# A graph kernel's last layer: source rows of three in seven cell groups fetched by indirect DMA in place of one-hot matmuls

## The chip, the cores and the metric

The kernel runs on one core of a Trainium2 chip. The metric is the device time of one execution in microseconds (us). The core has a matrix engine (TensorE, PE), a vector engine (VectorE, DVE), an activation engine (ScalarE, ACT), a general engine (GpSimd, POOL) and a queue engine (SyncE, SP). PE reads its operands from the on-chip memory SBUF and writes PSUM. DMA queues move data between DRAM and SBUF; SP, ACT and POOL issue them, and only POOL issues the indirect ones that fetch rows by index.

## What is computed

Four graph layers run one after the other on 3125 nodes of 128 features and 103125 edges (50000 random pairs in both directions, and a loop on each node). Each adds its result to x. The change is in the last:

```
h = relu(layernorm(x))
comp  = h[src] + rel_emb[rel_id]                 # one row of 128 per edge
score = sum(comp * h[dst], axis=-1)
smax  = segment_max(score, dst);  ex = exp(score - smax[dst])
norm  = ex / segment_sum(ex, dst)[dst]
neigh = segment_sum(comp * norm[:, None], dst)
x = x + tanh(neigh @ neigh_w)
```

All values are float32.

## The kernel before

**Cells.** The nodes are cut into T = 28 tiles of Q = 112. An edge belongs to the cell (tile of its source, tile of its target). Each cell has 128 slots, one per SBUF partition; edges beyond 128 go to OV = 3 overflow slots per partition of the target tile. `lay_out` sorts the edges into cells at the program's start. There `own` holds, for each slot, the source node's number in its tile, or -1 for an empty slot. `kind` and `rel` are further columns of the same layout, sent to DRAM or kept.

**Columns and groups.** The last layer works through 28 columns, one per target tile. A column has NG = 8 groups: seven groups of K = 4 cells (4 x 128 edges), and a last one that holds the overflow's 3 x 128 edges. `attend` does this, for the first layer (three hops) and for the last (one hop). Every group passes through the same steps:

- `s_load` (L800): the load of half a column's slot numbers, copied to 112 partitions (L774). `s_hot` (L826): DVE turns them into a one-hot matrix.
- `s_rel` (L834): SP loads the group's 4 x 128 relation rows (256 KB).
- `s_rows` (L836): PE makes the source rows. The features are kept as three bfloat16 parts whose sum is the float32 value, so each cell takes three matmuls, and a group 12 (L845). The rows land in a PSUM tile `pg`, of which there are two. For the overflow group the rows come from `over_rows` instead.
- `s_comb` (L853): DVE adds the relation rows, giving `v`.
- `s_turn` (L861, copied by ACT in L863): PE transposes v. `s_score` (L877): PE multiplies by the targets' features; DVE masks the product in L879, with `other` made by ACT (L1626) from `eq`, loaded by SP (L1621).
- `s_most` (L891): DVE keeps the running maximum of the column. After the last group PE turns it (L899), DVE reduces it and puts it on a diagonal (L905 to L908), PE spreads it over the partitions (L917) and ACT copies it (L919).
- `s_less` (L923, DVE), `s_exp` (L927, ACT) and `s_sum` (L935, PE): subtract the maximum, exponential, weighted sum of v per target.
- After a column: division (L1630 to L1634); after four columns a product with `neigh_w` (L1642), tanh, addition to x and the store of the output.

**Order.** The order of the work is written out by hand. The list `order` at the end of `attend` gives each step a delay in groups: at iteration i the step with delay d works on group i - d, and the steps of one iteration stand in the order of the list. `in_order` ties each engine's instructions to this order. So within an iteration PE does L935 (delay 21), L917 (11), L899 (10), L877 (8), L861 (6) and L845 (4). DVE does L923 (19), L891 (9), L853 (5), L879 (8), L905 to L908 (10) and L826 (2). `s_load` has delay 0.

**Gathers.** Where a row is fetched by index, `gather` (L708) has POOL issue an indirect DMA: 128 rows of 512 bytes, one for each partition. Before the change the last layer has three of them per column, for the overflow's rows (`s_over`, L814), 84 in all, into two buffers `orow`. They come from the table `rows_d` in DRAM, which SP writes from the normalised features at the layer's start (L1615). In the first layer's second and third hop POOL also fetches the relation rows for the last layer (`rel_ahead`, the tile `ahead`) and writes them to DRAM (L1012).

Of the kernel before, what the change touches and what calls it, by code (L numbers as in the profile page):

```python
# [7 lines left out]
F32 = mybir.dt.float32  # L8
BF16 = mybir.dt.bfloat16
FP16 = mybir.dt.float16  # L10
I32 = mybir.dt.int32
AF = mybir.ActivationFunctionType
OP = mybir.AluOpType
# [3 lines left out]
P = 128  # L17
D = 128
H, C = 4, 32
K = 4  # L20
# [3 lines left out]
Q = 112  # L24
# [418 lines left out]
def by_cells(ctx: ExitStack, tc: tile.TileContext, edges, x, E, edge_emb, q_w, k_w, Ws, Wd, att_s, att_d,  # L443
# [9 lines left out]
    nc = tc.nc  # L453
    N = x.shape[0]
    T = -(-N // Q)
# [5 lines left out]
    NG = T // K + 1  # L461
# [78 lines left out]
    overO = node.tile([P, 2, T, OV], F32, name="overO")  # L540
    n_src = node.tile([Q, T], F32, name="n_src")
    inO = node.tile([P, T, OV], I32, name="inO")
    slots_o = tc.dram_tile([2 * T * NO, 4], F32, name="slots_o")

    def rows_out(rb, to, width, by_dst):
# [11 lines left out]
    def lay_out(rows, tab, pp, pname):  # L557
# [11 lines left out]
        with tc.tile_pool(name="lay", bufs=1) as lp:  # L569
# [11 lines left out]
            for i in range(4):  # L581
                c = slice(i * W // 4, (i + 1) * W // 4)
# [3 lines left out]
            def flat(name, dtype=F32, n=W):  # L586
                return lp.tile([P, n], dtype, name=name)

            def split(f, bits):

                v = flat(f"v{f}")
                for j in range(2):
                    c = slice(j * WH, (j + 1) * WH)
                    nc.vector.tensor_add(v[:, c], layC[:, c, f], tab[2 * f + j][:, :WH])
                i = flat(f"i{f}", I32)
                nc.vector.tensor_scalar(i, v, 2.0 ** bits, None, op0=OP.mult)
                lo, hi = flat("lo", I32), flat("hi", I32)
                nc.vector.tensor_single_scalar(hi, i, bits + 7, op=OP.arith_shift_right)
                nc.vector.tensor_single_scalar(lo, i, bits, op=OP.arith_shift_right)
                hf, lf, at = flat(f"hf{f}"), flat(f"lf{f}"), flat(f"at{f}")  # L600
                nc.scalar.copy(hf, hi)
                nc.vector.tensor_scalar_add(lf, lo, -1.0)
                nc.vector.scalar_tensor_tensor(at, hf, -128.0, lf, op0=OP.mult, op1=OP.add)
                return v, i, hf, lf, at

            def row_tiles(f):

                n = f.shape[-1]
                w = min(n, Q)
                rb = lp.tile([w, n // w, P], BF16, name=f"rb{n}", bufs=2)  # L610
                for i0 in range(0, n // w, K):
                    m = min(K, n // w - i0)
                    pt = pp.tile([P, K, P], F32, name=pname)
                    for i in range(m):
                        nc.tensor.transpose(pt[:w, i, :], f[:, (i0 + i) * w:(i0 + i + 1) * w], ident)
                    nc.scalar.copy(rb[:, i0:i0 + m, :], pt[:w, :m, :])
                return rb

            def over_out(rb, to):
                o = bass.AP(tensor=to.tensor, offset=to.offset + T * P, ap=[[COL * P, T], [P, OV], [1, P]])  # L620
                nc.sync.dma_start(o, rb[:, 0, :])
# [8 lines left out]
            v0, _, k0, l0, own = split(0, 11)  # L630
# [8 lines left out]
            rows_out(row_tiles(kind[:, :NC]), src_kind, COL, False)  # L639
            over_out(row_tiles(kind[:, NC:]), src_kind)  # L640


            rel = flat("rel")
            nc.vector.tensor_sub(rel, v0, l0)
# [62 lines left out]
    def gather(to, table, index):  # L707
        return nc.gpsimd.indirect_dma_start(out=to, out_offset=None, in_=table,  # L708
                                            in_offset=bass.IndirectOffsetOnAxis(ap=index, axis=0))
# [4 lines left out]
    def norm_relu_steps(h):  # L714

        st = work.tile([Q, T, 6], F32, name="bn", bufs=1)
        mv = work.tile([Q, T, 2], F32, name="mv", bufs=1)
        for n0, n1 in quads():
            for n in range(n0, n1):
                nc.vector.bn_stats(st[:, n, :], xs[:, n, :])  # L720
                nc.vector.bn_aggr(mv[:, n, :], st[:, n, :])
            yield
        rs = work.tile([Q, T], F32, name="rs", bufs=1)
        nc.scalar.activation(rs, mv[:, :, 1], AF.Sqrt, bias=eps[:Q])
        nc.vector.reciprocal(rs, rs)
        for n0, n1 in quads():
            for n in range(n0, n1):
                nc.vector.tensor_scalar(h[:, n, :], xs[:, n, :], mv[:, n, 0:1], rs[:, n:n + 1],
                                        op0=OP.subtract, op1=OP.mult)
            nc.scalar.activation(h[:, n0:n1, :], h[:, n0:n1, :], AF.Relu)  # L730
            yield

    def norm_relu(h):
        for _ in norm_relu_steps(h):
            pass
# [41 lines left out]
    def width(g):  # L777
        return OV if g == NG - 1 else K


    def attend(oh_d, tables, idx, side, combine, rel_d, masks, finish, rel_rows=None, right=None, aside=None,
               column_end=None, extra=None):

# [7 lines left out]
        hop = 0  # L793
# [6 lines left out]
        def s_load(c, g):  # L800
            s = st[c, g] = {}
            m = width(g)
            if g % H1 == 0:
                h = cols[c, g // H1] = {}
                h["n"] = min(HALF if g == 0 else COL - HALF, T - g * K)
                h["oh"] = row_tile(oh_d, c, g * K, h["n"], name="oh")
            if g == 0:
                over_rows[c] = work.tile([P, OV, D], F32, name="orow", bufs=2)
            if rel_rows and not hop:
                rel_rows[0](s, c, g)  # L810
            if aside:
                aside(c * NG + g)

        def s_over(early, late):  # L814

# [20 lines left out]
        def s_rows(c, g):  # L836
            s, h = st[c, g], cols[c, g // H1]
            e0 = g % H1 * K
            if g == NG - 1:
                s["rows"] = over_rows.pop(c)  # L840
            else:
                pg = s["rows"] = pg_.tile([P, K, D], F32, name="pg")
                for k in range(K):
                    for i in range(3):
                        nc.tensor.matmul(pg[:, k, :], h["oh"][:, (e0 + k) * P:(e0 + k + 1) * P],  # L845
                                         parts[:, g * K + k, i, :D], start=(i == 0), stop=(i == 2))
            if rel_rows and not hop:
                rel_rows[2](s, c, g)
# [104 lines left out]
        with in_order(tc):  # L953
            for i in range(len(tables) * A - AFTER + 1 + order[0][1]):
                for f, d in order:
                    hop, u = divmod(i - d, A)
                    if 0 <= hop < len(tables) and u < T * NG:
                        f(*divmod(u, NG))
                hop, u = divmod(i, A)
# [12 lines left out]
    hop = 0  # L972
# [25 lines left out]
    with tc.tile_pool(name="work0", bufs=3) as work:  # L998
# [96 lines left out]
        tables = rows_d, rows_e, rows_d  # L1095
# [513 lines left out]

    with tc.tile_pool(name="work3", bufs=3) as work:  # L1610
        h = big.tile([Q, T, D], F32, name="agg")
        norm_relu(h)
        for n0, n1 in quads():
            in_parts(h, n0, n1)
        nc.sync.dma_start(node_rows(rows_d), h)  # L1615
        side = work.tile([P, T, Q], F32, name="side", bufs=1)
        sides(h, side)
        def other_load(s, c, g):
            m = width(g)
            s["eq"] = work.tile([P, K, Q], F32, name="eq", bufs=4)  # L1620
            nc.sync.dma_start(s["eq"][:, :m, :].rearrange("p k q -> p (k q)"), eq_d[c * NG + g, :, :m * Q])  # L1621

        def other_make(s, c, g):
            m = width(g)
            s["other"] = work.tile([P, K, Q], BF16, name="other", bufs=4)
            nc.scalar.activation(s["other"][:, :m, :], s["eq"][:, :m, :], AF.Copy, bias=1.0, scale=-1.0)  # L1626

        def weight(c, acc):
            r = over_one[c] = work.tile([Q, 1], F32, name="r", bufs=2)
            nc.vector.tensor_scalar_max(r, acc[:, D:D + 1], 1e-30)  # L1630
            nc.vector.reciprocal(r, r)

        def mean(c, acc):
            nc.scalar.activation(h[:, c, :], acc[:, :D], AF.Copy, scale=over_one.pop(c))  # L1634

        def turned(n0, n1):
            nexts[n0] = transposed(h, n0, n1)

        def by_w(n0, n1):
            pw = pm.tile([P, K, P], F32, name="pm")  # L1640
            for n in range(K):
                nc.tensor.matmul(pw[:Q, n, :], nexts[n0][:, n, :], nw, start=True, stop=True)  # L1642
            nexts[n0] = work.tile([Q, K, D], F32, name="th", bufs=2)
            nc.scalar.activation(nexts[n0], pw[:Q], AF.Tanh)

        def result(n0, n1):
            nc.vector.tensor_add(xs[:, n0:n1, :], xs[:, n0:n1, :], nexts.pop(n0))
            n = n1 - (n1 == T)
            nc.sync.dma_start(out[n0 * Q:n * Q, :].rearrange("(n p) d -> p n d", p=Q), xs[:, n0:n, :])
            if n1 == T:  # L1650
                nc.sync.dma_start(out[n * Q:, :], xs[:TAIL, n, :])

        attend(dst_oh, (rows_d,), inO, side, OP.add, dst_rel, (other_load, other_make, lambda *a: None),
               (weight, mean, *map(by_quads, (turned, by_w, result))))


@with_exitstack
# [701 lines left out]
```

## Time and profile before

| | |
|---|---|
| median of 3 runs | 7348.25 us (7346.42 to 7352.07) |
| profiled execution | 7342.68 us |
| its span, first to last instruction | 7340.9 us |
| mean granted TensorE clock | 0.913 |
| PE, DVE, ACT, POOL busy over the span | 85%, 75%, 52%, 50% |
| last layer | from about 6652 us to the end |
| gathers of the last layer (L708, orow) | 84, first 6678.9, 0.938 / 0.944 / 1.187 us (least, median, most) |

The page's shares are means over the whole program, of which the last layer is a tenth. So what follows is read in windows of that layer. In a table by windows each engine has its busy time and, in brackets, its number of instructions; then come the granted clock, the share of time in which the core's DMA engines were busy, and GB/s. In a timeline each row has the start, the duration, the engine, the line, the operation with output and inputs, and in brackets how long the engine sat idle before it and what ended this. A float32 matmul is recorded as two, so "x8" stands for four. DVE's and PE's operations overlap at their ends, so the time from one start to the next is what one costs in a train of them. In the list of waits each row has the total in us, the number of waits and the longest.

### The profile page before, as it was taken

How to read it: one execution, taken by the hardware profiler on the slowest of the kernel's cores; microseconds unless marked ns; L12 is line 12 of the kernel's file. 1: busy time of each engine (PE TensorE's matmuls, PEld its weight loads, DVE VectorE, ACT ScalarE, POOL GpSimd, SP SyncE). 2: the span in 40 equal slices, each digit the busy share in tenths (PEclk: the TensorE clock that was granted, in tenths of full speed). 3: DMA queues.
4: the chain of work that ended last, by engine and by line, in shares of the span. 5: the costliest groups of instructions: out<-in, count | busy, mean ns of one | idle time of the engine just before them, and what ended most of it. 6: DMA issues, size and time to landing. Idle time of an engine off the chain costs nothing.

```text
span 7340.9 us, 161470 instructions
## 1 busy us (share of the span) xinstructions
PE 6244.2 (85%) x59495; PEld 5200.1 (71%) x59495; DVE 5521.5 (75%) x12113; ACT 3838.1 (52%) x12186; POOL 3688.5 (50%) x3346
## 2 busy tenths in 40 slices
PE   5887739999999999999967777777877777988999
PEld 3443328888888888888856666666776776767999
DVE  8887638888866667777767878879997997237887
ACT  3666514444544445444556676655665666114555
POOL 2677767776568876888823333323342232341110
PEclk9787769999999999999978888888897898999999
DMA  2100025555467776766756766677777786556665
GB/s 65 26 19 17 12 62 150 149 149 150 146 193 207 204 207 185 206 204 200 205 168 204 213 209 212 210 203 204 209 209 195 209 210 179 146 150 185 211 210 170
DMA packets 695243, 1222.75 MB, mean 167 GB/s; under 512 B 129530, under 2 KB 459680, under 8 KB 694444
## 3 DMA queue, kind: packets, MB, share of 16 engines
q1 hardware_dynamic: 575340, 996.40, 46.1%
q0 software_dynamic: 109120, 208.86, 11.8%
q8 instruction: 473, 7.75, 0.5%
q10 hardware_dynamic: 9984, 7.07, 0.3%
q14 instruction: 326, 2.67, 0.1%
HBM read 915.61 MB, written 296.27 MB: 165 GB/s over the span
## 4 chain that ended last, share of the span: by engine, by line
PE 59%; DVE 10%; ACT 8%; DMA 4%; issue 3%; POOL 1%; ACTq 0%; SPq 0%; DVEq 0%; POOLq 0%
PE pa L935 11%; PE pm L877 10%; PE pm L869 7%; PE pg L845 7%; PE pa L1442 6%; DVE junk L1359 5%; PE pm L861 5%; ACT v L1428 3%; PE pg L1416 3%; PE pa L1550 2%; PE pm L1047 1%; DMA oh<-dst_oh 1%; ACT hot L1311 1%; PE pm L1340 1%; DMA eq<-eq_d 1%
## 5 line engine op out<-in xcount | busy, mean ns | idle before, releaser
L1359 DVE CUSTOM_DVE_ANT_0 junk<-arow,absent 112x1568 bf16<-112x1568 f32 x672 | 1231.9, 1833 | 10.8 <-DMA arow<-alpha_d 9.6
L708 POOL DMA_INDIRECT ahead<-in_L_gnn_rel_emb_dram,kindD x868 | 991.7, 1143 | 266.6 <-issue 256.6
L871 ACT ACTIVATE right<-pm 128x512 f32<-128x512 f32 (+1 forms) x672 | 392.0, 583 | 1196.1 <-PE pm L869 1196.0
L1442 PE MATMUL pa<-v,eq 128*112 128x132 f32 x5208 | 900.8, 316 | 122.5 <-ACT v L1433 34.3
L879 DVE SCALAR_TENSOR_TENSOR z<-other,pm 128x448 f32<-128x448 bf16 (+1 forms) x896 | 541.4, 604 | 576.3 <-PE pm L877 353.2
L935 PE MATMUL pa<-v,z 128*112 128x129 f32 x6944 | 951.0, 279 | 12.1 <-ACT z L927 12.0
L1442 PEld LDWEIGHTS pa<-v,eq 128*112 128x112 f32 x5208 | 733.4, 201 | 187.1 <-ACT v L1428 69.8
L935 PEld LDWEIGHTS pa<-v,z 128*112 128x112 f32 x6944 | 820.2, 177 | 34.1 <-ACT z L927 16.3
L373 POOL DMA_INDIRECT slots<-pay,pos x610 | 669.6, 1098 | 268.8 <-issue 183.5
L1428 ACT ACTIVATE v<-pg,w 128x32 f32<-128x32 f32 x3584 | 670.2, 343 | 203.6 <-PE pg L1416 193.3
L708 POOL DMA_INDIRECT orow<-gat_d,inO x252 | 375.3, 1489 | 798.1 <-DVE v L1430 310.5
L1416 PE MATMUL pg<-parts,oh 112*128 112x128 bf16 x7056 | 582.1, 232 | 170.2 <-DVE v L1430 127.8
L877 PE MATMUL pm<-side,right 128*128 128x112 f32 x5208 | 686.6, 275 | 7.7 <-DVE z L879 4.3
L869 PE MATMUL pm<-vT,kw 128*128 128x512 f32 (+1 forms) x1344 | 684.2, 591 | 0.2 <-DVE z L879 0.2
L861 PEld LDWEIGHTS pm<-ident,v 128*128 128x128 f32 x3472 | 430.3, 142 | 342.0 <-issue 272.6
L845 PE MATMUL pg<-parts,oh 112*128 112x128 bf16 x9408 | 659.1, 220 | 11.4 <-DVE oh L826 7.8
L863 ACT COPY vT<-pm 128x512 f32<-128x512 f32 (+1 forms) x896 | 510.8, 570 | 272.0 <-PE pm L861 198.9
L1416 PEld LDWEIGHTS <-oh 112*128 112x128 bf16 x7056 | 506.0, 105 | 202.5 <-issue 175.2
L877 PEld LDWEIGHTS pm<-side,right 128*128 128x128 f32 x5208 | 635.5, 192 | 10.4 <-issue 5.2
L708 POOL DMA_INDIRECT orow<-rows_d,inO x252 | 245.0, 972 | 734.4 <-DVE v L853 486.2
L845 PEld LDWEIGHTS <-oh 112*128 112x128 bf16 x9408 | 595.9, 98 | 21.7 <-issue 12.5
L1326 POOL TENSOR_TENSOR spread<-lo,hi 128x448 bf16<-128x448 bf16 x196 | 253.3, 1296 | 703.4 <-PE pm L1340 403.9
(384 smaller groups left out, 13567.8 us busy)
## 6 DMA issues: line engine op xcount, KB each, us to landing
eq<-eq_d SPq DMA_DIRECT2D x784, 224.0 KB
rel<-src_rel SPq DMA_DIRECT2D x392, 256.0 KB
dst_rel<-ahead POOLq DMA_DIRECT2D x196, 256.0 KB
rel<-dst_rel SPq DMA_DIRECT2D x196, 256.0 KB
other<-other_d SPq DMA_DIRECT2D x392, 112.0 KB
eq_d<-eqf SPq DMA_DIRECT2D x196, 224.0 KB
absent<-absent_d SPq DMA_DIRECT2D x56, 686.0 KB
ct<-count_d SPq DMA_DIRECT2D x56, 686.0 KB
```

Of the source, the lines that this page charges most:

```text
L373: st = nc.gpsimd.indirect_dma_start(out=slots, out_offset=bass.IndirectOffsetOnAxis(ap=pos[:m, k:k + 1], axis=0), in_=pay[:m, k0 + k, :], ...
L708: return nc.gpsimd.indirect_dma_start(out=to, out_offset=None, in_=table, in_offset=bass.IndirectOffsetOnAxis(ap=index, axis=0))
L845: nc.tensor.matmul(pg[:, k, :], h["oh"][:, (e0 + k) * P:(e0 + k + 1) * P], parts[:, g * K + k, i, :D], start=(i == 0), stop=(i == 2))
L861: nc.tensor.transpose(pT[:, k, :], s["v"][:, k, :D], ident)
L869: nc.tensor.matmul(pK[:, :m, :], right, s["vT"][:, :m, :], start=True, stop=True)
L877: nc.tensor.matmul(pS[:, k, :], s["vT"][:, k, :], side[:, c, :], start=True, stop=True)
L879: nc.vector.scalar_tensor_tensor(s["z"], s.pop("other")[:, :m, :], MASK, pS[:, :m, :], op0=OP.mult, op1=OP.add)
L935: nc.tensor.matmul(acc[:Q, :D + 1], s["z"][:, k, :], s["v"][:, k, :], start=(g == 0 and k == 0), stop=(g == NG - 1 and k == m - 1))
L1359: nc.vector.tensor_tensor_reduce(junk, arow[:, hd, half], c["absent"][:, half], 1.0, -3e38, OP.subtract, OP.max, accum_out=c["am"][:, j, h ...
L1416: nc.tensor.matmul(pg[:, k, :], c["oh", g * K // HALF][:, (e0 + k) * P:(e0 + k + 1) * P], parts[:, g * K + k, i, :D], start=(i == 0), stop ...
L1428: nc.scalar.activation(s["v"][:, k, o], s["rows"][:, k, o], AF.Copy, scale=w[:, k, hd:hd + 1])
L1442: nc.tensor.matmul(acc, s["eq"][:, k, :], s["v"][:, k, :], start=(g == 0 and k == 0), stop=(g == NG - 1 and k == m - 1))
```

## The change

In the last layer the rows of groups 1, 3 and 5 of each column are no longer made by PE. When such a group is loaded (delay 0), POOL issues four gathers from `rows_d` into one of four new SBUF tiles `fetched`, and `s_comb` reads that tile in place of `pg`. Groups 0, 2, 4 and 6 stay with PE, and so does the one-hot matrix of the whole column. The indices are made once, in `lay_out`: `own`, raised to 0 where a slot is empty, plus the tile's first node, as integers. They are stored to DRAM (`inC_d`) and loaded again at the last layer's start.

```diff
+    inC_d = tc.dram_tile([P, 3 * T * K], I32, name="inC_d")
...
+            srcs = lp.tile([P, T, K], F32, name="srcs")
+            inC = lp.tile([P, 3, T, K], I32, name="inC")
+            for j in range(3):
+                for k in range(K):
+                    s = (2 * j + 1) * K + k
+                    nc.vector.tensor_scalar(srcs[:, :, k], own[:, s * T:(s + 1) * T], 0.0, float(s * Q),
+                                            op0=OP.max, op1=OP.add)
+                nc.vector.tensor_copy(inC[:, j], srcs)
+            nc.scalar.dma_start(inC_d, inC.rearrange("p j t k -> p (j t k)"))
...
+            if fetched is not None and g % 2 and g < NG - 1:
+                s["rows"] = work.tile([P, K, D], F32, name="fetched", bufs=4)
+                for k in range(K):
+                    gather(s["rows"][:, k, :], tables[hop], fetched[:, g // 2, c, k:k + 1])
...
             if g == NG - 1:
                 s["rows"] = over_rows.pop(c)
-            else:
+            elif "rows" not in s:
                 pg = s["rows"] = pg_.tile([P, K, D], F32, name="pg")
...
+        inC = work.tile([P, 3, T, K], I32, name="inC", bufs=1)
+        nc.scalar.dma_start(inC.rearrange("p j t k -> p (j t k)"), inC_d)
...
-               (weight, mean, *map(by_quads, (turned, by_w, result))))
+               (weight, mean, *map(by_quads, (turned, by_w, result))), fetched=inC)
```

The step `s_load`, in which the gathers stand, comes behind the other steps in the order of an iteration; `s_over` for column 0 has delay 10, for column 1 delay 4, and for the later columns 0.

More of the change, by code (lines that the diff above doesn't have):

```diff
@@ L781, in attend @@
     def attend(oh_d, tables, idx, side, combine, rel_d, masks, finish, rel_rows=None, right=None, aside=None,
-               column_end=None, extra=None):
+               column_end=None, extra=None, fetched=None):
         nonlocal hop
```

## The prediction, before the result was known

> **What bounds the kernel now.** I first read the 40 slices to find the last layer (from 6652 us), then the table by windows inside it.
>
> ```profile
> core 0: us, PE busy (x) PEld busy (x) DVE busy (x) ACT busy (x) POOL busy (x), PEclk, DMA share, GB/s
> 6750.00:6800.00 50.00, 50.00 (x537) 49.61 (x536) 43.13 (x87) 27.14 (x58) 6.68 (x7) 1.00 0.68 211
> ```
>
> TensorE is busy all 50 of 50 us at full clock, DVE 86%, POOL 13%, DMA 0.68. So PE sets this layer and POOL is nearly free. That speaks for the change. Next, the waits of 6700 to 7300:
>
> ```profile
> POOL orow L708 <- DVE v L853: 484.2, 25, 20.5
> DVE z L879 <- PE pm L877: 66.2, 84, 1.7
> PE pm L917 <- DVE diag L908: 1.2, 1, 1.2
> ```
>
> PE waits for almost nothing; POOL waits 484 us for a buffer. A column ends every 22.9 us (23.5 where four columns are written out), 23.2 on average. Third, the timeline of one column's end:
>
> ```profile
> 6720.94 1.04 PE L877 MATMUL pm<-side,vT 128*128 128x112 f32 x8
> 6721.82 0.60 PE L861 MATMUL pm<-ident,v 128*128 128x128 f32 x4
> 6722.26 0.84 PE L845 MATMUL pg<-parts,oh 112*128 112x128 bf16 x12
> 6722.63 0.68 DVE L905 TENSOR_REDUCE mx<-pm 112x1 f32<-112x512 f32 x1
> 6722.93 1.09 PE L935 MATMUL pa<-v,z 128*112 128x129 f32 x8
> 6723.54 0.28 DVE L908 TENSOR_SCALAR diag<-ident,mx 112x112 f32<-112x112 f32 x1
> 6723.97 0.45 PE L917 MATMUL pm<-diag,ones 112*128 112x112 f32 x2
> ```
>
> Start to start, a group's twelve row matmuls take 0.67 us (6722.26 to 6722.93). DVE's chain (score, mask, maximum, diag) ends at 6723.82, just before PE is through with its own queue and spreads the maximum (L917). Last, how a gather runs on POOL beside DVE, in the second hop of the first layer and in the last layer:
>
> ```profile
> 3024.73 0.61 DVE L826 TENSOR_SCALAR oh<-oh,iota_p 112x1536 bf16<-112x1536 bf16 x1
> 3025.16 2.10 POOL L708 DMA_INDIRECT ahead<-in_L_gnn_rel_emb_dram,kindD  x1 [0.30 <-issue]
> 3025.26 0.62 DVE L923 TENSOR_TENSOR z<-z,row_m 128x448 f32<-128x448 f32 x1
> 3025.80 0.62 DVE L891 TENSOR_TENSOR most<-most,z 128x448 f32<-128x448 f32 x1
> 3026.33 0.68 DVE L853 TENSOR_TENSOR v<-pg,rel 128x512 f32<-128x512 f32 x1
> ...
> 6916.34 0.94 POOL L708 DMA_INDIRECT orow<-rows_d,inO  x1 [20.46 <-DVE v L853]
> 6916.79 0.60 DVE L923 TENSOR_TENSOR z<-z,row_m 128x448 f32<-128x448 f32 x1
> ```
>
> A gather takes 0.94 us, but 2.10 when L923 and L891 start just after it: it ends 0.93 after L891 gives way to L853, which reads PSUM. A DVE operation with both inputs in SBUF holds a gather up. Over the hops (2100 to 3650) gathers whose first 0.2 us ends inside L923 average 1.65, inside L891 1.24, inside L826, L879 or nothing 0.95 to 0.99; all together 1.13.
>
> **Removed.** 3 groups x 28 columns = 84 groups x 12 = 1008 matmuls; 84 x 0.67 = 56 us of PE, 2.01 per column. The one-hot loads and compares (L774, L826) stay.
>
> The saving is not whole. Group 5's matmuls of the next column are those at 6722.26, between score and spread. From score to spread DVE needs 3.03 us less 0.09 slack; PE without them needs 2.25. PE then waits for diag, and 0.58 of that 0.67 is lost. PE alone would need 23.2 - 2.01 + 0.58 = 21.8 us per column.
>
> **Added: 336 gathers.** POOL has 12 more per column beside the 3 for the overflow: 15. Alone each costs 0.94 + 0.30 to the next = 1.24 us; 15 x 1.24 = 18.7, which would hide under 21.8. But DVE's two-input operations stand against it. Start to start L923 and L891 take 0.53 each. L853 on a fetched group now has both inputs in SBUF (like the orow form, 0.55 busy); it costs DVE no more than the 0.68 from PSUM, but it too can hold POOL. Per column that makes four blocks of about 1.5 us (L923, L891 and L853 of the three fetched groups and of the overflow), three of 1.06 and one of 0.53. A train of period P met at random by a block B is delayed B²/2P if B < P, else B - P/2: 0.88, 0.45, 0.11. Sum 4 x 0.88 + 3 x 0.45 + 0.11 = 5.0. So 23.7 us per column, 1.58 per gather. The same formula for the hop (3.7 us per column of 15.5 gathers, POOL engaged 0.83 of the time) gives 0.20 per gather; 0.19 was measured. Laying a train of gathers over the DVE rows of 6740 to 7290, with these L853 counted as blocking, I get 1.64. From below: 1.52 if L853 doesn't block; from above 1.69, if each tile's arrival releases DVE's block just when the next gather asks. I take 1.60: 24.0 us per column, more than PE's 21.8. POOL becomes the bound. Its new waits: a gather waits for L853 of the tile four before it, long done when POOL is late; L853 waits for its tile, with L879 queued behind it on DVE and the transposes (L861) on PE, so all engines follow POOL.
>
> The Trainium skill (SBUF — State Buffer, "Who interferes with whom") says that a DVE instruction with two SBUF inputs contends with a GpSimd instruction that reads SBUF, that copies and tensor_scalars in the two-port modes do too, and that whoever is second blocks for the whole instruction. The first part is what the rows show, and it speaks against this change. The second isn't: gathers beside L826 (bf16 in SBUF) average 0.99. By the rule L826's 0.75 and 0.61 would add 0.4 per column (10 us in all); by the row nothing, which I take. Nor does a gather hold DVE for all its length: L923 at 6916.79 takes its 0.60 inside one.
>
> **Start of the layer.** The gathers read rows_d, written by the DMA issued at 6669.79 (L1615); the first gather ran at 6678.85. Until then PE has begun groups 0 to 2 today; now group 1 waits. POOL's queue order is groups 1, 3, 5 of column 0, group 1 of column 1, and only then column 0's overflow: 19th gather. At 1.25 and 1.65 us from a gather's end to its use (1042.63 to 1044.28, rel_g) group 7 is combined at about 6704 instead of 6687.6. So POOL is behind from the beginning and stays so.
>
> **The sum.** The last fetched group (27, 5) is POOL's 420th gather. The first 41, before L923 runs, at 1.3: 53. The other 379 at 1.60: 606. 6678.85 + 53 + 606 + 1.65 = 7340. Today this group is combined at 7304.5. What follows is the same queue of work, so the end moves by +36. Break-even is 1.506 us per gather.
>
> **Elsewhere.** At the layout (1018 to 1033) DVE gets 12 small operations and 3 copies, ACT's queue a 168 KB store. Small neighbours (84 elements) start 0.12 apart: about 1.7 us. DVE then idles 4.5 us for the src_kind store, which hides it; uncovered it and the store's landing cost 2. I take 1. The 168 KB load at the layer's start is ahead of need by 20 us: 0. DMA: 12 gathers x 32 packets at 148 ns (3.7% of 16 x 600 us for 2400 packets) = 3.6 us per column beside 16.2 now; 19.8 of 24 stays under the bound, and the loads have three groups of lead: 0, up to 10 if they are late.
>
> Profiled execution: 7342.7 (span 7340.9 and 1.8 around it) + 36 + 1 = 7380. The median of the runs is 5.6 above that execution: 7385.
>
> **Rivals.** *PE stays the bound* (faster): the gathers of the last layer average 1.01 today, so 15 x 1.31 = 19.7 and POOL keeps up after a late start. PE saves 75 groups x 0.67 less 25 x 0.58 = 36 after the start, loses 14 to 16 in it, 1 at the layout: 7348 - 20 = 7328. Against it: those gathers run in threes set off by L853, after L891 is through; a train doesn't choose its moment. It decides if a gather stays under 1.45. *Near a tie*: L853 doesn't block, 1.50 to 1.53, and POOL's loss eats PE's gain: 7349 to 7360. *DMA bound*: at PE's 21.8 the share would be 0.91, with bursts at the one-hot loads (0.97 in one 5.8 us window now); late rel loads on top of a slow POOL: over 7418. That the change doesn't do what it says: the index of an empty slot is clamped to a real row and masked later, so the number of rows moved is fixed; no time hangs on it.
>
> **Chances.** POOL bound 0.66 (7360 to 7418), tie 0.14, PE bound 0.12, worse 0.08. About 0.2%, 14.7 us, is what can be told from no change. Faster 0.12 (PE bound), same 0.18 (the tie and POOL's lowest end), slower 0.70. Range 7336 to 7418, leaving out the PE-bound case below and the worst above.
>
> **What would show it.** Right: POOL over 75% busy to the end, gathers of 1.2 us or more on average, DVE's L853 waiting for DMA "fetched", PE at 85 to 90%, columns 24 us apart. Wrong: gathers near 1.0 and PE still at 50 of 50; then L917 should wait 0.6 us per column for diag. If L853 waits for rel instead, it was DMA.

## The result, and the profile after

| | before | after |
|---|---|---|
| median of 5 runs each, taken side by side | 7346.42 us (7343.89 to 7352.07) | 7416.28 us (7408.78 to 7423.17) |
| profiled execution (span) | 7342.68 us (7340.9) | 7423.17 us (7421.4) |
| mean granted clock | 0.913 | 0.908 |

The change makes the kernel slower: ratio 1.0093 (95% interval 1.0081 to 1.0105), +70 us at the median. The forecast was 7385, slower, range 7336 to 7418.

In the changed kernel the lines stand lower: the gather L708 is L718, L826 is L840, L853 is L867, L861 is L875, L877 and L879 are L891 and L893, L891 is L905, L908 is L922, L917 is L931, L923 is L937.

First the table by windows of the changed kernel, a long stretch of the last layer and 50 us out of its middle. The columns are those shown before: window, its length, PE, PEld, DVE, ACT and POOL busy, clock, DMA share, GB/s.

```profile
6760.00:7260.00 500.00, 435.25 (x4155) 421.83 (x4154) 384.70 (x752) 248.74 (x519) 409.93 (x296) 0.98 0.73 224
6950.00:7000.00 50.00, 43.28 (x418) 41.38 (x416) 38.56 (x76) 24.94 (x52) 41.23 (x29) 1.00 0.74 227
```

PE, full before, now stands still for 13% of the time; DVE fell too. POOL rose from 13% to 82%. What fills the rest of POOL's time is in the waits of 6700 to 7300:

```profile
...
DVE v L867 <- DMA fetched<-rows_d,inC: 100.3, 45, 7.4
POOL fetched L718 <- issue: 77.3, 253, 0.3
PE pm L875 <- DVE v L867: 37.0, 44, 3.6
...
PE pm L931 <- DVE diag L922: 20.6, 22, 1.4
```

POOL's idle time before a gather is 0.3 us, 253 times, and nothing released it: that is the step from one gather to the next. Its long waits for a buffer (484 us before) are gone. POOL works without a pause and everybody follows: DVE waits for the fetched tile, PE for DVE. The first row names a DMA, but that alone doesn't convict the transfer: a tile can only land after POOL has issued it. Which of the two is late has to be shown by experiment.

Why POOL needs so long is in the timeline of POOL and DVE in the middle of the layer:

```profile
6960.22 0.89 DVE L840 TENSOR_SCALAR oh<-oh,iota_p 112x2048 bf16<-112x2048 bf16 x1
6960.89 2.09 POOL L718 DMA_INDIRECT fetched<-rows_d,inC  x1 [0.31 <-issue]
6961.02 0.60 DVE L937 TENSOR_TENSOR z<-z,row_m 128x448 f32<-128x448 f32 x1
6961.55 0.61 DVE L905 TENSOR_TENSOR most<-most,z 128x448 f32<-128x448 f32 x1
6962.09 0.68 DVE L867 TENSOR_TENSOR v<-pg,rel 128x512 f32<-128x512 f32 x1
6962.69 0.60 DVE L893 SCALAR_TENSOR_TENSOR z<-other,pm 128x448 f32<-128x448 bf16 x1
...
6963.22 0.61 DVE L937 TENSOR_TENSOR z<-z,row_m 128x448 f32<-128x448 f32 x1
6963.28 2.37 POOL L718 DMA_INDIRECT fetched<-rows_d,inC  x1 [0.30 <-issue]
6963.75 0.61 DVE L905 TENSOR_TENSOR most<-most,z 128x448 f32<-128x448 f32 x1
6964.29 0.55 DVE L867 TENSOR_TENSOR v<-orow,rel 128x384 f32<-128x384 f32 x1
6964.76 0.61 DVE L893 SCALAR_TENSOR_TENSOR z<-other,pm 128x448 f32<-128x448 bf16 x1
```

The first gather starts in the last 0.13 us of L840, the one-hot compare, and then meets L937 and L905, whose inputs lie in SBUF. It ends at 6962.98, 0.89 us after DVE has gone on to L867, which reads `pg` in PSUM. The second starts inside L937 and meets L905 and an L867 that reads `orow` in SBUF: three in a row. It ends at 6965.65, again 0.89 after DVE goes on to L893, which reads PSUM. L937, L905 and the L867 of `orow` keep their usual 0.55 to 0.61. So a held gather takes about its own 0.94 us counted from the moment at which DVE stops reading two inputs from SBUF.

What catches a gather is an operation that is already running when it starts. In the last layers of all ten profiles of this document, 779 gathers start inside an operation with two SBUF inputs, at least 0.06 us behind its start and 0.12 before its end, and all 779 are held. Another 310 start up to 0.6 us ahead of such an operation, behind one that reads PSUM, and none of them is.

To compare kernels, the last layer is measured from the issue of the `rows_d` store (6669.79 before, 6677.24 after) to the start of the combination of group (27, 5). A column is the mean over 15 columns of the middle; the spacing is from the start of one gather to the start of the next where POOL waited for nothing (6760 to 7240):

| | before | after |
|---|---|---|
| layer, store to (27, 5) | 634.7 us | 710.0 us |
| store to the combination of group (2, 5) | 54.9 | 77.5 |
| column | 23.22 | 25.32 (25.2 to 25.7 over other stretches of 15) |
| mean gather; spacing | 1.01; 1.35 (in threes) | 1.36; 1.69 |

Of the +75.3 us, 22.6 arise in the first three columns and 52.7 in the other 25.

### The profile page after: what moved, and what is told of

The parts are those of the page before. It is cut to its first block, busy times and chain, and to the rows that moved or that the text cites. A ratio compares the mean times of both kernels' runs of the same rounds, so it can differ in the third digit from the quotient of the medians.

```text
span 7421.4 us, 159888 instructions
## 1 busy us (share of the span) xinstructions
PE 6215.5 (84%) x58487; PEld 5171.8 (70%) x58487; DVE 5525.2 (74%) x12128; ACT 3837.7 (52%) x12186; POOL 4175.4 (56%) x3682
## 4 chain that ended last, share of the span: by engine, by line
PE 51%; DVE 12%; ACT 8%; DMA 6%; POOL 5%; issue 5%; ACTq 0%; DVEq 0%; SPq 0%; POOLq 0%
PE pa L949 8%; PE pm L891 8%; PE pm L883 7%; DVE junk L1373 6%; PE pa L1456 5%; PE pg L859 5%; PE pm L875 4%; ACT v L1442 3%; PE pg L1430 3%; PE pa L1564 2%; POOL fetched L718 2%; DMA fetched<-rows_d,inC 2%; DMA oh<-dst_oh 1%; POOL orow L718 1%; PE pm L1061 1%
## 5 line engine op out<-in xcount | busy, mean ns | idle before, releaser
L718 POOL DMA_INDIRECT ahead<-in_L_gnn_rel_emb_dram,kindD x868 | 990.3, 1141 | 264.9 <-issue 251.8
L893 DVE SCALAR_TENSOR_TENSOR z<-other,pm 128x448 f32<-128x448 bf16 (+1 forms) x896 | 539.8, 602 | 503.1 <-PE pm L891 291.3
L718 POOL DMA_INDIRECT orow<-gat_d,inO x252 | 375.8, 1491 | 804.1 <-DVE v L1444 316.4
L875 PEld LDWEIGHTS pm<-ident,v 128*128 128x128 f32 x3472 | 430.8, 143 | 427.3 <-issue 313.2
L1430 PE MATMUL pg<-parts,oh 112*128 112x128 bf16 x7056 | 586.2, 233 | 164.7 <-DVE v L1444 126.7
L891 PE MATMUL pm<-side,right 128*128 128x112 f32 x5208 | 685.7, 274 | 5.5 <-ACT right L885 3.4
L877 ACT COPY vT<-pm 128x512 f32<-128x512 f32 (+1 forms) x896 | 510.8, 570 | 341.1 <-PE pm L875 308.4
L1430 PEld LDWEIGHTS <-oh 112*128 112x128 bf16 x7056 | 509.9, 106 | 195.4 <-issue 167.9
L891 PEld LDWEIGHTS pm<-side,right 128*128 128x128 f32 x5208 | 634.9, 192 | 8.2 <-ACT right L885 4.7
L859 PE MATMUL pg<-parts,oh 112*128 112x128 bf16 x8400 | 592.4, 220 | 12.0 <-DVE oh L840 8.3
L875 PE MATMUL pm<-ident,v 128*128 128x128 f32 x3472 | 536.8, 276 | 77.3 <-DVE v L867 54.3
L859 PEld LDWEIGHTS <-oh 112*128 112x128 bf16 x8400 | 536.1, 98 | 21.5 <-issue 13.1
```

Source lines behind the costliest of these rows:

```text
L875: nc.tensor.transpose(pT[:, k, :], s["v"][:, k, :D], ident)
L891: nc.tensor.matmul(pS[:, k, :], s["vT"][:, k, :], side[:, c, :], start=True, stop=True)
L893: nc.vector.scalar_tensor_tensor(s["z"], s.pop("other")[:, :m, :], MASK, pS[:, :m, :], op0=OP.mult, op1=OP.add)
L1430: nc.tensor.matmul(pg[:, k, :], c["oh", g * K // HALF][:, (e0 + k) * P:(e0 + k + 1) * P], parts[:, g * K + k, i, :D], start=(i == 0), stop ...
```

## The experiments

Theory A: gathers are held up by DVE operations with two SBUF inputs, so POOL's own rate, 15 gathers per column, sets the column. Theory B: the transfers set it (more packets, landings late). Within A it was open why the spacing was 1.69 and not the 1.52 worked out with L867 not counted: L867's own second SBUF input, or a lock-step in which each tile's arrival sends off DVE's block just as the next gather starts. Further, what PE's relief is worth by itself.

| kernel | ratio (95% interval) | layer | column | spacing | DMA share |
|---|---|---|---|---|---|
| after | 1.0093 (1.0081 to 1.0105) | 710.0 | 25.32 | 1.69 | 0.73 |
| 1 row in PSUM | 0.9979 (0.9971 to 0.9986) | 618.8 | 21.78 | 1.34 | 0.87 |
| 2 gathers unused, rows by PE | 0.9991 (0.9981 to 1.0001) | 634.4 | 23.25 | 1.52 | 0.82 |
| 3 no gathers, no matmuls | 0.9946 (0.9928 to 0.9963) | 598.9 | 21.80 | | 0.73 |
| 4 two groups | 0.9961 (0.9947 to 0.9975) | 613.9 | 21.81 | 1.62 | 0.83 |
| 5 gathers unused, rows from a constant in SBUF | 1.0080 (1.0065 to 1.0096) | 698.2 | 25.69 | 1.70 | 0.73 |
| 6 three groups, from column 2 on | 1.0042 (1.0029 to 1.0055) | 678.4 | 25.21 | 1.69 | 0.73 |
| 7 two groups, from column 2 on | 0.9936 (0.9922 to 0.9950) | 600.4 | 21.81 | 1.61 | 0.82 |
| 8 groups 1, 3, 6 from column 2 on, row in PSUM | 0.9929 (0.9916 to 0.9943) | 579.8 | 21.09 | 1.41 | 0.88 |

The ratios are to the kernel before on the same chip (its medians 7350.55 us for 1 to 4, 7347.35 for 5 to 8). Layer, column and spacing are us, each from one profiled execution; the DMA share is that of 6760 to 7260. Against the ranges expected for the medians: 1, 4, 6 and 8 lie inside theirs, 2, 3 and 5 miss by 1.4 to 3.5 us, and 7 is 6.4 us faster than its own.

**1. One input of L937 in PSUM.** All gathers stay. PE's spread maximum is left in PSUM, in an unused part of the tile `pa`, so L937 reads one input from there; ACT's copy goes.

```diff
         def s_spread_most(c, g):
...
+            if fetched is not None:
+                acc = cols[c]["acc"] = pa_.tile([P, 512], F32, name="pa")
+                cols[c]["row"] = acc[:, 256:256 + Q]
+                nc.tensor.matmul(cols[c]["row"], ones[:Q, :], cols[c]["diag"], start=True, stop=True)
+                return
...
```

> The kernel after, but in the last layer the spread maximum stays in PSUM (a free part of the column's sum bank), so that the subtraction L923 of before has one input in SBUF and not two; ACT's copy of it (0.25 us a column) falls away. Theory A, DVE's operations with two SBUF inputs hold POOL's gathers up: of each column's blocks the eight subtractions (0.53 each) go, four blocks of about 1.06 and three or four of 0.53 are left, delays by the random-phase formula 4 x 0.45 + 3 x 0.11 = 2.1 us; gathers average about 1.08 in place of 1.36, 15 take 20.8 us, under PE's 21.8, and the time falls to 7330 to 7350. Theory B, the gathers are slow because the DMA engines (busy 0.73) give their descriptors back late: the mean gather stays at 1.35 or more and the time at 7410 to 7420.

7333.09 us. The group rows of the gather, first of the changed kernel, then of this one, give least, median and most in ns, and the first and last start:

```profile
L718 POOL DMA_INDIRECT fetched<-rows_d,inC x336: 940/1344/2497, 6690.4 to 7383.3; - x168
```

```profile
L718 POOL DMA_INDIRECT fetched<-rows_d,inC x336: 940/944/2011, 6677.7 to 7265.0; - x168
```

The median gather falls from 1.34 us to the undisturbed 0.94, the mean of all 420 from 1.36 to 1.03. The same rows are moved, in less time, at a DMA share of 0.87 in place of 0.73. That contradicts B and is what A says. The waits of this kernel (6760 to 7260) show what binds now:

```profile
...
POOL orow L718 <- DVE v L867: 35.0, 18, 3.2
...
PEld pa L933 <- DVE diag L922: 18.4, 23, 1.1
PE pa L933 <- DVE diag L922: 13.7, 23, 0.9
```

POOL again waits for a buffer, so it isn't the bound any more. PE waits 0.6 us per column (13.7 / 23) for DVE's `diag` (L933 is the spread in this kernel). The start still costs: store to group (2, 5) is 75.4 us.

**2. Gathers that nobody uses.** PE makes all rows, the gathers land in a spare tile.

```diff
-                s["rows"] = work.tile([P, K, D], F32, name="fetched", bufs=4)
+                spare = work.tile([P, K, D], F32, name="fetched", bufs=4)
                 for k in range(K):
-                    gather(s["rows"][:, k, :], tables[hop], fetched[:, g // 2, c, k:k + 1])
+                    gather(spare[:, k, :], tables[hop], fetched[:, g // 2, c, k:k + 1])
```

> The kernel after with all its gathers, but PE makes the rows of all seven groups as before, and L853 reads them from PSUM; what the gathers fetch is used by nobody. Theory A: L853 no longer has two SBUF inputs on the fetched groups and nobody waits for POOL; the gathers average about 1.2 (1.52 from one to the next), 15 take 22.8 us, just under the 23.2 of PE, so the layer runs as before: 7345 to 7360. Theory B: same DMA traffic, so gathers stay at 1.35 or more, but as nobody waits for them the time is as before plus what the loads lose to them, 7345 to 7365. A third, C, that the slow gathers come of the lock-step between a tile's arrival and DVE's burst of work after it: the gathers average about 1.0 to 1.1 here.

7343.64 us, no difference from before. By windows, first the kernel before, then this one:

```profile
6760.00:7260.00 500.00, 500.00 (x5346) 495.77 (x5345) 423.06 (x825) 273.65 (x571) 63.86 (x63) 1.00 0.69 211
```

```profile
6760.00:7260.00 500.00, 499.88 (x5349) 495.51 (x5348) 427.29 (x826) 273.58 (x572) 399.72 (x330) 1.00 0.82 246
```

PE is full again, and the columns come 23.25 us apart: 336 more gathers and their traffic cost PE and the loads nothing that shows; DVE is busy 4 us longer in 500. POOL runs its train at 1.52 per gather: with L867 of these groups reading PSUM, the train has the lower end of the forecast.

**3. PE's relief alone.** No gathers for groups 1, 3, 5 and no matmuls either: their source rows are a constant tile in SBUF. So the source rows of these groups are left out of the computation.

```diff
+            still = work.tile([P, K, D], F32, name="still", bufs=1)
+            nc.vector.memset(still, 0.5)
...
-                s["rows"] = work.tile([P, K, D], F32, name="fetched", bufs=4)
-                for k in range(K):
-                    gather(s["rows"][:, k, :], tables[hop], fetched[:, g // 2, c, k:k + 1])
+                s["rows"] = still
```

> The kernel after without its gathers: groups 1, 3 and 5 of a column take their source rows from one constant tile in SBUF (so those rows' real values are left out). It shows PE's saving alone. If my account of the path is right, PE gets 21.8 us per column, waits about 0.6 us for the diagonal at each column's end, and the time falls by 27 x 1.43 = 39: 7305 to 7312. If PE's whole 56 us were to be had: 7290. If DVE or DMA took over at once: 7325 or more.

7313.54 us; the layer is 35.8 us shorter than before, a column 21.80. Of the waits of 6760 to 7260 one row matters (L932 is the spread, L923 `diag` here):

```profile
PE pm L932 <- DVE diag L923: 15.0, 23, 0.7
```

15.0 / 23 = 0.65 us per column: the matmuls of group 5 did hide DVE's chain to the maximum, and PE gets 23.22 - 21.80 = 1.42 of the 2.01 that it no longer works.

**4. Two groups.** As changed, with `g in (1, 3)` in the condition; PE makes group 5.

> Only groups 1 and 3 fetched, group 5 again by PE. Theory A: POOL has 11 gathers per column, at 1.55 to 1.65 each 17 to 18 us, under PE's 23.2 - 1.34 = 21.9; PE is the bound again and waits for nothing at the diagonal; saving 26 x 1.34 = 35 less 6 to 10 at the layer's start: 7315 to 7325. Theory B, DMA: the gathers' bytes fall by a third, POOL under the bound too, so the same within 10 us. If the loss of the change were one at the layer's start alone, and not POOL's pace, this would lose two thirds of it: 7390.

7323.63 us. 11 gathers x 1.62 = 17.8 us fit under PE's column of 21.81, and PE is busy 500.00 of 500. Two groups give PE as much as three without gathers (21.80): the third group's matmuls only turned into the wait for `diag`.

**5. L867's input, or lock-step.** Groups 1, 3, 5 are combined from a constant SBUF tile that is always there, as in experiment 3; the gathers run as in experiment 2. So no L867 of these groups waits for a landing, but each reads two inputs from SBUF. Their source rows are left out.

```diff
...
-                s["rows"] = work.tile([P, K, D], F32, name="fetched", bufs=4)
+                s["rows"] = still
+                spare = work.tile([P, K, D], F32, name="fetched", bufs=4)
                 for k in range(K):
-                    gather(s["rows"][:, k, :], tables[hop], fetched[:, g // 2, c, k:k + 1])
+                    gather(spare[:, k, :], tables[hop], fetched[:, g // 2, c, k:k + 1])
```

> All gathers of the change are issued and used by nobody, and groups 1, 3 and 5 take their rows from one constant SBUF tile (their real values are left out), so that L853 has two SBUF inputs as in the change but never waits for a tile. It parts two causes of the slow gathers. If L853's second SBUF input makes the difference to the run with PSUM rows (1.20 us a gather, 1.52 from one to the next), gathers average about 1.33, as in the change, a column's 15 take 24.5 us, and the overflow's gathers, which stand in the same queue, still hold the layer: 7385 to 7410. If it is the waiting (a tile's arrival releasing DVE just as the next gather asks), gathers stay at about 1.20, 15 take 22.8 us a column, and the time is 7335 to 7350.

7413.54 us, like the change itself. Its waits of 6760 to 7260 (L871 is the combination here):

```profile
...
DVE v L871 <- DMA orow<-rows_d,inO: 93.1, 19, 6.1
```

The spacing is 1.70, with no landing of a fetched tile to fall into step with. So L867's second SBUF input takes the train from 1.52 to 1.70, and lock-step with landings isn't needed for it. Experiments 2 and 5 also differ in PE's matmuls, but 4 and 7, with two such groups per column beside a full PE, lie between, at 1.62 and 1.61. POOL stays the bound even so: the overflow's gathers, three of every 15, stand in the same queue, and DVE waits for them once a column (15 x 1.70 = 25.5 us against 25.69).

**6. A later start.** The condition is `c >= 2 and g % 2 and g < NG - 1`: PE makes all rows of the first two columns.

> The change, but columns 0 and 1 make all their rows by PE and the fetching begins with column 2, when the table has long been stored. POOL then begins with a lead of four tiles. If the start's 20 us (the 21st group is combined 20 us later in the change, counted from the table's store) come on top of POOL's pace, the time falls by up to 20: 7390 to 7400; if POOL's pace alone sets the end, it falls by the two columns' gathers less what four columns at PE's pace cost: 24 gathers x 1.69 = 40 at most, so not below 7370.

7377.26 us: still slower than before, less so than the change. The layer takes 678.4 us, 31.6 less than with the change, and the spacing stays 1.69. By group (2, 5) it is 22.8 us ahead of the change (54.7 against 77.5), as the layer no longer waits for POOL's first gathers, and by (4, 5) 32.4 (97.6 against 130.0): columns 3 and 4 still take 21.5 and 21.4 us while POOL uses up its lead. From there on both go at POOL's pace, and that alone keeps it slower than before.

**7 and 8. Towards a better version.** 7: `c >= 2 and g in (1, 3)`. 8: experiment 1's edit with `c >= 2 and g in (1, 3, 6)`, and the indices laid out for group 6 instead of 5. Group 5 stays with PE, in front of the spread.

> Groups 1 and 3 only, and from column 2 on. POOL keeps up (11 gathers, 18 us of 21.8), PE is the bound, and the late start (14 us at the 21st group in the run with groups 1 and 3 of all columns) is gone: 26 x 1.34 = 35 less than before: 7310 to 7318.

> Spread maximum kept in PSUM, and groups 1, 3 and 6 fetched from column 2 on: group 6 in place of 5, since PE's rows of group 5 stand between score and spread, where they hide DVE's chain. PE then saves all of 2.01 us per column, 26 x 2.01 = 52; POOL needs 15 x 1.35 to 1.40 = 21 us of PE's 21.2, so just keeps up; DVE is at 93%. 7295 to 7305. If the diagonal still costs PE its 0.6 per column, 7312.

7 gives 7303.57 us, 8 gives 7298.26, and both beat the kernel before. The windows of 8:

```profile
6760.00:7260.00 500.00, 499.72 (x5035) 496.35 (x5034) 469.71 (x908) 295.02 (x606) 380.35 (x345) 1.00 0.88 269
```

PE is full and gets 23.22 - 21.09 = 2.13 us per column, the whole saving (2.01 by the forecast's count). POOL is no further from its limit: 15 x 1.41 = 21.1 us, so a fourth group would have nothing to hide under.

## Why the prediction was right, and where its sizes were off

**POOL becomes the bound: shown.** POOL 82% busy to the layer's end, gathers 1.36 us on average, L867 waiting for `fetched`, PE at 87%: four of the five signs that were named. The fifth, the column, is 25.3 us and not 24. In experiments 1, 2 and 5 the gathers' time follows the place of DVE's inputs. This is the rule of the Trainium skill on DVE instructions with two SBUF inputs (SBUF — State Buffer, "Who interferes with whom"), with this case's price on it: the spacing is 1.69 with L937, L905 and L867 in SBUF, 1.52 with L867 in PSUM, 1.34 with L937 in PSUM. That section also has whoever comes second block for the whole instruction, which it says of the two-port modes; for two SBUF inputs the rows show it of the gather alone. In the changed kernel 35 L937 and L905 start inside a gather that keeps its 0.94, and none of them takes over 0.62.

**PE's side: right.** 2.01 us less 0.58 for `diag` was to give 21.8 per column; experiment 3 gives 21.80 and a wait of 0.65.

**The mis-sized term: 1.60 per gather.** The median, 7416.28, lies 1.7 us inside the upper end of the range: the forecast was +37 and the measured loss is +70. Measured to (27, 5) from the store's issue, the forecast says 7340 - 6669.79 = 670 and the changed kernel 710.0. By its terms:

| term | forecast | measured |
|---|---|---|
| store to the first gather | 9.1 | 9.2 |
| first 41 gathers | 53 | 58.0 |
| the other 379 | 606 (1.60 each) | 640.1 (1.69 each) |
| from the last to its use | 1.65 | 2.8 |

So 34 of the 40 us lie in one number. The range reached far enough because its upper end is about what 1.69 gives (7385 + 34 = 7419), but 1.69 had been argued from lock-step with landings, which experiment 5 sets aside. In that the hit was lucky. Two things were left out of the middle value.

The first is L826, the one-hot compare (L840 after), which the prediction put at nothing, against what the same section of the Trainium skill says of tensor_scalars in the two-port modes, that they contend as well. (No trace names the mode in which L826 ran.) The reason given was that gathers beside it average 0.99. That average counted a gather as beside L826 when the point 0.2 us after its start lay in L826, and so took in gathers that start ahead of it and left out those that start near its end. Sorted by the start itself, in the same stretch of the kernel before (2100 to 3650), 50 gathers start in L826 (0.06 us or more behind its start): 49 are held, and the 50 average 2.00 us. The 39 that start from 0.2 ahead to 0.06 behind average 0.95. The gather of 3025.16 that the prediction shows starts inside L826 as well, and ahead of L923. Experiment 1 has the plainest case, since there the operation behind L840 reads PSUM:

```profile
6719.92 0.75 DVE L840 TENSOR_SCALAR oh<-oh,iota_p 112x2048 bf16<-112x2048 bf16 x1
6720.11 1.37 POOL L718 DMA_INDIRECT fetched<-rows_d,inC  x1 [0.31 <-issue]
6720.58 0.61 DVE L942 TENSOR_TENSOR z<-z,pa 128x448 f32<-128x448 f32 x1
```

The gather ends at 6721.48, 0.90 us after DVE has left L840 for L942. In the last layer L840 nearly always stands right ahead of L937 (45 of 48 times in the changed kernel), so the two make one longer block. By the prediction's own formula, blocks longer by 0.53 and 0.66 us add 1.2 us per column: 18.6 (15 x 1.24, not 18.7) + 5.0 + 1.2 = 24.8, or 1.65 per gather in place of 1.58. That the formula without L826 agreed with the hop (0.20 against 0.19) was luck: these 50 gathers alone make 53 of the 182 us of hold-up there.

The second is the random meeting that the formula assumes. A held gather ends 0.89 us after its block and the next starts 0.30 later, 1.19 in all; in the timeline above L867 and L893 take 1.13 (6962.09 to 6963.22), so the next gather starts when the next L937 has just begun. Counted over the changed kernel's rows (6760 to 7240, 283 gathers), the blocks as they stand would give by the formula 84 us of hold-up without L840 and 109 with it, and 126 were measured: 1.54, 1.63 and 1.69 per gather. Blocks of L937 and L905 alone catch a gather 98% of the time and hold it for 0.67 us on average, where the formula says 0.47. This working is from traces; no run takes L840 out of the way.

A reading of the kernel before was off too, without weight: a column in which four are written out takes 24.1 us, not 23.5 (the mean of 23.2 is right).

**The start: nearly right in size, wrong in order.** The prediction and the description of the order ahead of it said that column 0's overflow is fetched 19th, by delays of 10 and 4. That is a misreading. The last layer has one hop, in which the condition of `s_over` leaves only the entry with delay 0, for every column: the overflow comes first. In the timeline:

```profile
6686.41 1.23 POOL L718 DMA_INDIRECT orow<-rows_d,inO  x1 [26.00 <-DMA eq<-eq_d]
...
6694.19 0.94 POOL L718 DMA_INDIRECT fetched<-rows_d,inC  x1 [0.30 <-issue]
...
6696.87 0.69 DVE L867 TENSOR_TENSOR v<-fetched,rel 128x512 f32<-128x512 f32 x1 [10.06 <-DMA fetched<-rows_d,inC]
...
6697.71 1.09 PE L875 MATMUL pm<-ident,v 128*128 128x128 f32 x4 [13.57 <-DVE v L867]
```

The first gather is one of `orow`; the fourth of group 1 starts at 6694.19, and 1.74 us after its end DVE combines the group, after 10 us of waiting, PE 13.6. With either order POOL is late from the first column on, so the sum, which only counts gathers, hardly changes. What is lost in the first three columns is 22.6 us; experiments 6 and 7 get it back by leaving two columns to PE.

**DMA at nothing: right.** Experiments 2, 1 and 8 move the gathers' traffic (in 8, but for two columns) at shares of 0.82 to 0.88 without PE or DVE being late for it. The rival that the layer ends later for late loads falls.

**The layout: +1 forecast, nothing seen.** The first hop's first matmul starts at 1040.56 instead of 1041.47, 0.9 us earlier.

**The sum against the runs.** +75 in the layer beside +70 at the medians. The store that opens the layer was issued between 6663.7 and 6686.3 over the profiled executions of all these kernels; only differences inside the layer were read.

## What to carry to other kernels

An idle POOL isn't free for indirect gathers: price one beside the DVE operations that it will run among, and count each DVE operation whose inputs both lie in SBUF, also those that the change itself moves there, and a tensor_scalar like the one-hot compare here. To see what holds a gather, look at what is running when it starts. When the gathers' rate times their number passes the column of the present bound, fetch fewer (two groups gave PE the same as three), or leave one input of a DVE operation in PSUM, which here turned 1.69 us per gather into 1.34. And let a new source of work start where it has a lead, not in the first columns of a layer whose table has just been written.

## What the runs showed of the hardware that was not expected

One input of one DVE operation is worth 0.18 to 0.35 us per gather: a SBUF input more in three of 8 combinations took the spacing from 1.52 to 1.70, one fewer in each L937 from 1.69 to 1.34. Whether a gather of 0.94 us becomes one of 2 us is settled within some hundredths of a microsecond, by what DVE is running at its start. For two SBUF inputs the hold-up is one-sided: gathers stretch up to 2.50 us in the layer's middle, while L937 and L905 keep 0.49 to 0.63 (before 0.50 to 0.62). With the one-hot compare it goes both ways: it holds gathers, and beside them it takes up to 0.89 us (112x2048) in place of 0.75. And unused gathers, 12 per column with 786 KB of rows, cost the kernel nothing that could be measured (0.9991, interval 0.9981 to 1.0001), though POOL's train of 15 x 1.52 = 22.8 us only just fits the column of 23.25.
